# Three edits and a new order in a one-core transformer block: shared score tile for two query blocks, scaling within the centring, comparisons on VectorE

## The chip, the core and the metric

The kernel runs on one core of one Trainium2 chip. Its time is the device time of one execution in microseconds. The engines are TensorE (PE in the profile, PEld for its weight loads), VectorE (DVE), ScalarE (ACT), GpSimd (POOL) and SyncE (SP), which issues all the DMAs here. An engine runs its instructions strictly in the order of the program.

## The reference

A transformer block on x of shape (8, 512, 512): attention with 16 heads of 32, then a feed-forward part of two "bit-linear" layers with 2048 hidden columns.

```python
qkv = layernorm(x) @ w_attn + b_attn          # q, k, v; 16 heads of 32; q and k rotated by head
scores = einsum('bhtd,bhsd->bhts', q, k)       # causal: -inf above the diagonal
attn = softmax(scores) * E ** -0.5
x = x + layernorm((attn @ v) @ w_proj + b_proj)

def bitlinear(x, w):
    xn = layer_norm(x)
    g = max(abs(xn))                           # of a row
    x_hat = clip(xn * 128 / g, ...) * g / 128  # no rounding
    w_hat = sign(round(w / mean(abs(w)))) * mean(abs(w))   # -1, 0, 1 times one number
    return x_hat @ w_hat.T
h = gelu(bitlinear(layernorm(x), w_fc))        # 512 -> 2048
x = x + layernorm(bitlinear(h, w_proj))        # 2048 -> 512
```

## The kernel before

Rows are handled in blocks of 128: 8 batches of 4 blocks give 32 blocks. To keep accuracy, a float32 operand of a matmul is split into two float16 halves, a rounded one ("cast") and what is left of it (the "remainder").

The program consists of some twenty streams, each a Python generator that issues a few instructions per step. `ORDER` is a string of 4519 letters; each letter runs the next step of its stream, and every engine keeps exactly that order. So which instruction stands before which on an engine is read from the string.

- `w`, `H`, `J`, `B`, `R`: load and prepare the attention weights. `t`, `T`: load the feed-forward weights in 16 pieces of 128x1024 (twice), and sum their magnitudes. `Y`: thresholds, then for each piece (`ternarize`) two steps: `neg = w < -half` on GpSimd (L443) and `(w > half) - neg` into fp8 on VectorE (L445).
- `n`, `N`: load and normalise a block of x, split and transpose it. `Q`, `V`: queries and keys of four heads (L551, L565), values (L521, L536). One query and key step group is 12 steps.
- `S` (`maxima`): scores of four heads and one of the four query blocks. Query block i sees (i+1)x128 keys. Each unit claims two of the three PSUM tiles of the pool `sc` (2 banks each); twelve matmuls fill them (L583), then VectorE adds the mask, copies to the tile `p` and reduces (L595, two per tile), and adds the two parts of the shift (L605). 12 steps for the four blocks.
- `A` (`probabilities`): Exp on ScalarE (L627), the cast (L632), the remainder on GpSimd (L634), and for blocks 0 to 2 together and for block 3 a transposing DMA (`pT`). 28 steps for the four blocks.
- `W`: attention weights times values (L661), with the end on VectorE (L674 to L680). `G`: split and transpose the result. `P`: project (L706), with normalisation and residual.
- `F`: normalise, scale, split and transpose the rows for the first layer. `X`: the first layer (L782) and Gelu (L791). `Z` (`ff_quantise`, 15 steps a block): mean, centring on GpSimd (L808), largest magnitude (L810), sum of squares on ScalarE (L815), then, with the scale known, cast (L738) and remainder (L740, VectorE) of each half and its transposing DMA. `C`: the second layer (L838, 8 steps of 4 matmuls), normalisation, residual, store.

Small reciprocal square roots run on GpSimd (L151) and stand in the same queue as its large instructions.

Of the kernel before, what the change touches and what calls it, by code (L numbers as in the profile page):

```python
# [10 lines left out]
F32 = mybir.dt.float32  # L11
# [24 lines left out]
nnwwwNBNNnwnttHtJJHHNNHHHNHHwNNBBJINBRJBNBBJBTHNBHHHNJNBTNTBHNNNHNNNwNBRNHtTtTttJJJHHttRRRRwBTNN  # L36
NBtTHNBBNBRRHHTBttTtYRRJTtYTtYTNtNNQJJJJJNTtJRNHQQHJJQTJTwQQQQTYYYYQJHJHHYHttQtQQnSQYQYSSwQYtYtt
QYSHSAYAANSAAtYAAAnAQQQNJYtQQQQQSVAASVJJAJVJAASHSAAAAAQAQQQYVQVNSQAAASVQVQVHSSVVQAAVAVQQQAAAASAS
VSYJVVtVVVVYAVSSVVAAAASAVVVYYAVAAJtVSSQQQQWVWWnnAAQAQWWWAAAQQQNQVVNNNANSNNNNSWWWWWWAAAAAAQANVNAN
WANNWSnSAVAARSSSAAAASSSWYYAAtAVNANSVWWWWSAAAAAAAAWNQNSSGGWWWWWWYYNYAnAAAAAAWVVVWSVSVVQQQVSAAAAAA  # L40
AAQGQSYSGAAASAAGAQSRVRSrWVVAAWtWWtWQSAQWVWSSQQWYRAAWWVYQWSQAAWVWWSYGSAYAAAVAAAAARSQQQQQQQQAQQQSQ
SWtAAAAASASAYWWWGYGAAVAGAWSWWWWWWWWWASAVSGGSVGVQAAAQQAAQAAASAAPYSQPAAAPtPQSPSQASSQAQQAVQVPQFAAVW
WVSVAVFAAVVVAFnSrAYASAPANWPSFWPVPNVSVQFQFWQAWnAQFAAAAAPWWQQQQQQNNNNNWNNSSPNFWWWAAAAAAAASSNWNNAAA
AWGFSAAAPPPNSSNXPPXAAAXXSAFQSSSNANVAVWFFAXrWWWWWXXXXQGNFnWAAAXASQSYYZWZWWNWWAAAAQXSWVZQVAFZZWZAA
XXQYXQQAXXQXPAZZQAnXQSXXPFSQQSQPrSSPPPFANWWWWWWAAGASSGVVrGWAAASWWWWAAAAZAAZAAAZWVSVVZVWWSQQVVSQS
PQAAAAAAAAAQSZQAZZZZSQQAQQVAASQQSFVVVAAAWWCCCASVSAASWGWWGWSGAAAWZSCWCVWCGWWWWAAAAAZAFVFVNSQQSWSQ
NZAAAAQFSSAAACQQAACCSSCCAAQGZZQFZQQQQFVVVVGWGASVAAnWVAVVVWASWWWWCAAArPSSAVAAZCZZFPSWWPWWWWVWVAAA
AXPPXXSSQAASAZAZAAAFAZZQAAAACQXQQFCXQAFnXCXXQXSQQQNNXPNFANCQSSZZNNANNAAAAAASCFWQSCWNNNANACAWWZZn
GCSCCPSSPWWCSGWNPAWWAPAAVNNWNWACXrWPWVAVVVVVWVVVAAAFZSVSVAAXZQZZAXAQVQVQXZVQPFSAAAAVZQZPPFSPFQSS
FFFFAPPFFAAAQAAXXXXQSSXZZCZZFFFFAXPAZZCXQQQSCAZAZZZFZZNAAFFZXCZZZZZZPCPXCXCXAXACXCCCXSSSXCPPPGGG  # L50
WWWWWGWXSSZWAQCAASCCCAAQWWWWWWWACCZSAZFAAAASSAQAACQQCSZZZQFAAAAASAGCCCSZACQQSCZQAQSrAWWWWQWWGWVQ
VCWWWrAWAWAWCWAAAGVGPGVFGZXNASAZVXVXVZFVAVSAXPVXASFPFXAVVAPQZSPPQZSSQAFXAAAAQQQQXQZSZANXCSQCQnPA
AASCWWWAWAWWCFFXQAZAQZFVSZWSCVCAAAAASWSAAVVCWCNFPCZWWZWPSAPACCQnAWZZZQWAPQZXAAZFQXXQCQFAQXQGGSQC
QrSZZANZNPNAAZZAAAXAFXXXACXSSSCXZZXQQSNNSCVCWCWVCWWWWFACAZNZNAZZAAAZXCZSWWWXnFPWNZCWWWAAAnFANNNN
CFNAAVVXXXZWPCXXZSXCPVZPZNNZCXNrSXPNSSXAANZPCVSAAAAAAVCAVCZZCSAASCZVZSZCZAAAAAAVVAAAZFZZCCVVSSCV
VSCXCWXWQWQWnWWQZZPZSVFZPQZAAAPAAAXSQFQPGGGAFQPGQSXQZCrASXFQAAAACWAXFSAQPAXCSWWWWCWQQPCFQWXCAZZA
SAZAZWSSZAZAACSQAACQAZZCFSWCQQQWQWWWnFSWQAAANFXGGQCWXWXWWAZCSAAAAZZFNCQFGFAQWXAWXWCrCWAAXFVFXSFS
ZXVXSGVVVSZQGVXQAFQAZXZVGAZAVASQQQQXSAQVQSZAAAAAAZQQXVFZXSQPFZVVPWPPAZSAZAZCZWFFPCVCZZWWWCWPFXWF
FZCVCAASSAASACACCAZAZZXCCAAASSXXXCACAVVPXSPZSSQAArPQZZPPAAAAAQQQZQSCZFFWWWZWWAACQAWSSQZWZCQPCAQN
NAAAAASQQAAAAGANCXGCFNSNNNSZCCSCXWVWWWZWWWCCNVWWXZWWWWWAXAnAAnPVVZZSSPSZAVAAPVPNVSVAANNFSNCrCASC  # L60
CNAAAAAAANNNFFAAAXAAPNXCXCXCXVCVFZXSVSCFXSZSFSXCVWQXFWQXQAZAZWWWWCAPAACZSAZACPZAXXQPCCZXZrXFZFQA
ZZPGGZGQWXQXSQPQWWZZZSNWFGAPWCASQAACAAAQAZAZAASCFSWCWQCVWSCAZSSFZZACVAAAACVVCXCSQCQSQAZAAAFnAGQS
ZGQQZGQQPnWWQWWAWSQWAAAAAACWVWWWWWWWArXNVZSNQXCFFQGGAGSSAVAXVPZSSZQQQPAASFAAXAAQQPXFAQPFQXQSQPVA
QZSAXVXAWAWAQAQVZZSXZVVAZVSAZVVCVAWFWCSWACWZZFFZVCZWVWZWCWWVWWAAAPZSZCWZZSAAAASnAAZASCXZZCXXASQA
QQCCCAAAACQQQQCXXQACQCQNNNCACXNSSCSFNQCNNAFANNFQPACPANNANAAAFSSNCPPAFSZCPSAXXCCXASGGAWWrWWWWAAVX
WSNVNnWWWWZWWSNAAZAFWAFVVVXVSXXSQXZZAZAAZVVAAAAZZZSZZACrAAQQQQAZQSPPAZZAAAAXXPXZXQPQNPFAXQCAPCXS
QFSCQZXPZCSSXAQAVCSVZZZZAXAZACZSAAVVXZZCPSZFAAPAFCZSPWXCWXWWWPWXXZASAnAZGZCFCGGFCCFWWXWCWCWFWFAX
PSQASSCFQZGWWQAAAAAAACZQCSQQCSAAAAQQZSSQFANAArASWQQFQCFGWCASZAZVCCVWWWVVGWWWGWVWWAWWCCWVAAAAVVVC
SrCASFASVVVVAXZZPGGAGVAZVVXSQAXSAQPQXPAFAAFFZZSQPFZAZAAANNAQQAXXPXXQPZZZXFFXPZQZPQSSQSQQPFSPZWPn
CWWAAAAAWWCAnWPCSVSSVCAAWAAAAAZAVSSXCZVSQQQQAAAZAAZXZCZAQASZZZQQWQWWQWQNNANCSZZNNNNNWQXQAWWAAAFA  # L70
ANNACCXCNNNACXCANCCCCCSSAAACSASAACZFSASCAVCCXSXSXWWWWWWNAAANXAGGSWWWWWWWVrAXSCFACQAQVAFFWZFFVASA
PQXQQQQXZASQAZPAQAAASSSPQZPXAZQQAAAPAAZVSPZSAFVVZVAAVCAArSXZVXXZCFVZZVPZZVFXXVVXXVXZPXZSSXPWWXCW
FZAZZZCAZPGCXWCPCGGWCZZZSZWZZCXZCXXZPWZGSAXAACAAAAAACCCCAQCSWWCWWWCQFWXCZSSZCQCAAAAACAFCZZZFFWQG
AFFSWSZZSAZWWWQCWWCQVrACGGSWQVQXQACACASSZZXXAAAQSWAWZAASZAWAAXAAQXAAXWFWXWQZXFWXZVFVSQFQGXCZPZAS
AQSWZQQQFCrSACQAWAQACFAFAAQZSCGQGQCFCZZQVSAVCZAAAAWWWWVZZVPCCXZFAPWFFAASPFSZXZPPXVSAAZPXXXFFVCZX
XAACVPXZPSVCCrPXFZXPFSZZFSCXCXAASPQAXZCQCQCAZZZFQAFZZSWWAWAACZZZZZXZXPCWFXQXWQSXAFFAPWACAZFXFFCC
FPSPPCWAAAZAASPSrZCQWQZZZZWAQQAAQQCAASZZSSACAPCZPWCWSAZSWCWACCCZAASSAGGWCPAAAPSAWWWAPWWWCCCAAZAG
SAXAAVWXXVASZZASAFFSAAGAAXAVXXArAXCXFXSPXZCCCZWWCZASCVWWZWWZZZZCSZGWAGXAASZZZAASAAAFAASAXCCSXFZS
SXFAAAZZCPWAWWZWFWAAAAAAAAWAFFCWCXFGCCCXCXXXCCXZZFFZZZXZCXXGFFWCXXXWXWWWWCWWWWWWWrGWZGGXGCCXZXZZ
ZZCZXXXZZZPZCXXXCCPPZZPPZPFXPFFCXrCFZFPZCPFZCPCXXPPFCPCZZZZZPXZZCXXPXZZXXPCFCCCrCCZPFFXFCXFCXZZZ  # L80
ZZZCPFFZXPFCFZZZPZZZFFCXZCXCCXZCPCXXPXFZZZZFFZZPCrCZCPXZFZFCXCZXXXFFCZXZCZXCZXFZXCZXZZFZFZZZZZZC
CCCZCCCXXCXXCXCXCXZCZZZZZZZZZZZZZXXCXCZCZCCCCCXCXCXXZZCZZZZCCZCZZZZZCCCZCZCZCCCCCCCCCCCCCCCCCCCC
CCCCCCC
# [4 lines left out]
def block_kernel(  # L88
# [349 lines left out]
    def ternarize(n, i):  # L438
        dst = piece((wfc, wout)[n], i)
        t = pcs.pop((n, i, 1))  # L440
        half, nhalf = thr[n]
        neg = tp.tile(list(dst.shape), BF16, tag="q", name="neg", bufs=2)
        nc.gpsimd.tensor_scalar(neg, t, nhalf, None, ALU.is_lt)  # L443
        yield
        nc.vector.scalar_tensor_tensor(  # L445
            dst, t, half, neg, ALU.is_gt, ALU.subtract, saturate=False
        )
        yield
# [119 lines left out]

    def maxima(u):

        b, g = divmod(u, NG)
        src = srcs.pop((b, g))
        low = lows[u % 2]
        nm = small.tile([P, NT, 4], F32, tag="nmax", name="nmax")
        for i in range(NT):
            n = (i + 1) * P
            scs = [sc_tile(), sc_tile()]
            for m, (hq, hk) in enumerate(((0, 3), (2, 3), (0, 1))):  # L580
                for j in range(4):
                    rows = slice(j * HD, (j + 1) * HD)
                    nc.tensor.matmul(  # L583
                        scs[j // 2][:, j % 2, :n],
                        src[rows, hq, ts(i, P)],
                        src[rows, hk, :n],
                        start=(m == 0),
                        stop=(m == 2),
                    )
            yield  # L590
            for t in range(2):
                p = pp.tile([P, 2, n], F32, tag="p", name="p", bufs=3)
                scores[2 * u + t, i] = p, nm[:, i, 2 * t : 2 * t + 2]
                for j in range(2):
                    nc.vector.tensor_tensor_reduce(  # L595
                        p[:, j, :],
                        scs[t][:, j, :n],
                        mask[:, T - n :],
                        e_scale[:, g : g + 1],
                        3.0e38,  # L600
                        ALU.add,
                        ALU.min,
                        low[:, i, 2 * t + j, 0:1],
                    )
                nc.vector.tensor_reduce(  # L605
                    nm[:, i, 2 * t : 2 * t + 2], low[:, i, 2 * t : 2 * t + 2], AX.X, ALU.add
                )
                yield

# [5 lines left out]
    def probabilities(u):  # L615

        qs = {}
        for i in range(NT):
            part = PARTS[i]
            for t in range(2):  # L620
                if STARTS[i] == 0:
                    shape = [P, 2, 2, BLOCKS[part] * P]
                    qs[t] = pp.tile(shape, F16, tag=f"ph{part}", name="ph", bufs=2)
                q = qs[t]
                p, add = scores.pop((2 * u + t, i))
                for j in range(2):
                    nc.scalar.activation(  # L627
                        p[:, j, :], p[:, j, :], AF.Exp, bias=add[:, j : j + 1], scale=-1.0
                    )
                yield  # L630
# [368 lines left out]
```

## Time and profile before

| | |
|---|---|
| runs | 1089.4, 1091.85, 1092.23 us; median 1091.85 us |
| profiled execution, its own time | 1095.54 us |
| its span, first to last instruction | 1093.7 us |
| mean granted TensorE clock | 0.973 |
| busy: PE, DVE, ACT, POOL | 987.7, 965.6, 870.4, 766.7 us |
| matmuls | 8170 |
| DMA traffic | 189.77 MB, mean 174 GB/s |

PE's busy time is modelled from pipelined matmuls, so a matmul's own duration (381 ns for 512 columns) is longer than the distance to the next one. In a waits list a line names who waited, for whom, the sum in us, how often and the longest. In a timeline a line gives the start, the length, the engine, the line of the kernel, the operation, what it writes and reads, and how many; in brackets stands the idle time before it and what ended it. L-numbers are lines of the kernel before.

### The profile page before, as it was taken

To read this page: it belongs to the slowest core of one execution; us is meant where nothing else is said; L and a number is where in the kernel's file an instruction comes from. 1 tells how busy PE (TensorE), PEld (TensorE's weight loads), DVE (VectorE), ACT (ScalarE), POOL (GpSimd) and SP (SyncE) were. 2 spreads that over 40 slices of the span, in tenths; PEclk is the share of its full clock that TensorE was granted. 3 is DMA by queue.
4 is the path that set the end of the run, shared out by engine and by line. 5 is a ranking of instruction groups with operands and counts; after the bars stand their busy time and mean duration, and the time that the engine had idled before them with its cause. 6 is when DMAs were issued, how large, how long until landed. Compare 5 with 4: busy or idle time off the path is not lost. (4 is left out here: it accounts for less than half of the span.)

```text
span 1093.7 us, 23185 instructions
## 1 busy us (share of the span) xinstructions
PE 987.7 (90%) x8170; PEld 502.3 (46%) x8170; DVE 965.6 (88%) x2859; ACT 870.4 (80%) x1439; POOL 766.7 (70%) x678
## 2 busy tenths in 40 slices
PE   2668577898999999999999999999999999999996
PEld 1325334445454554545454554445454444444442
DVE  6988889998989998999799988999999989987964
ACT  4747777698888898998879898998899879974551
POOL 6888998887785767866577858777784666763533
PEclk9889799999999999999999999999999999999999
DMA  9657998999998999998799999999997989995653
GB/s 311 215 187 161 180 209 156 191 173 171 185 169 165 176 191 170 188 188 160 145 179 190 189 159 188 174 184 166 181 181 164 173 155 160 167 195 112 136 108 89
DMA packets 588501, 189.77 MB, mean 174 GB/s; under 512 B 564576, under 2 KB 568672, under 8 KB 588384
## 3 DMA queue, kind: packets, MB, share of 16 engines
q1 hardware_dynamic: 588384, 188.28, 88.6%
q8 instruction: 64, 1.05, 0.4%
q14 instruction: 53, 0.43, 0.1%
HBM read 38.29 MB, written 8.39 MB: 43 GB/s over the span
## 5 line engine op out<-in xcount | busy, mean ns | idle before, releaser
L634 POOL TENSOR_TENSOR ph<-p,ph 128x256 f16<-128x256 f32 (+3 forms) x256 | 372.4, 1461 | 128.7 <-ACT ph L632 109.2
L627 ACT ACTIVATE p<-p,nmax 128x384 f32<-128x384 f32 (+3 forms) x512 | 258.3, 552 | 36.1 <-DVE nmax L605 34.2
L595 DVE CUSTOM_DVE_ANT_0 p<-sc,mask,e_scale 128x384 f32<-128x384 f32 (+3 forms) x512 | 260.0, 545 | 16.7 <-PE sc L583 8.7
L838 PE MATMUL mm<-wout,qT 128*128 128x512 fp8e4 x1024 | 256.6, 381 | 3.4 <-DMA qT<-q 3.2
L782 PE MATMUL sc<-wfc,qT 128*128 128x512 fp8e4 x1024 | 255.8, 381 | 2.4 <-ACT h L791 2.1
L551 PE MATMUL mm<-xT,wqk 128*128 128x512 f16 x768 | 202.4, 391 | 6.3 <-DVE sc L676 2.5
L632 ACT CAST ph<-p 128x256 f16<-128x256 f32 (+3 forms) x256 | 184.8, 722 | 10.3 <-DMA pT<-ph 4.3
L782 PEld LDWEIGHTS <-qT 128*128 128x128 f16 x1024 | 96.8, 98 | 116.4 <-issue 12.3
L838 PEld LDWEIGHTS <-qT 128*128 128x128 f16 x1024 | 94.6, 98 | 110.1 <-issue 6.7
L661 PEld LDWEIGHTS <-pT 128*128 128x128 f16 x2560 | 94.0, 97 | 54.1 <-issue 14.3
L551 PEld LDWEIGHTS <-wqk 128*128 128x128 f16 x768 | 71.4, 100 | 96.0 <-issue 25.6
L661 PE MATMUL sc<-vt,pT 128*128 128x65 f16 (+1 forms) x2560 | 97.5, 187 | 17.3 <-DMA pT<-ph 8.5
L521 PE MATMUL mm<-wv,xT 128*128 128x256 f16 x768 | 104.8, 280 | 7.5 <-DVE src L565 4.9
L583 PE MATMUL sc<-src 32*128 32x128 f16 (+3 forms) x1536 | 86.2, 303 | 26.6 <-DVE low L595 16.1
L706 PE MATMUL mm<-wp,oT 128*128 128x512 f16 x384 | 103.1, 384 | 0.8 <-DMA oT<-hT 0.8
L740 DVE SCALAR_TENSOR_TENSOR q<-h,hqs,q 128x1024 f16<-128x1024 f32 x64 | 84.7, 1333 | 10.0 <-ACT q L738 9.9
L808 POOL TENSOR_SCALAR h<-h,hnm 128x1024 f32<-128x1024 f32 x64 | 74.5, 1168 | 26.7 <-DVE hnm L803 25.3
L521 PEld LDWEIGHTS <-xT 128*128 128x128 f16 x768 | 74.5, 100 | 35.4 <-issue 13.5
L791 ACT ACTIVATE h<-sc,fsc 128x1024 f32<-128x1024 f32 x64 | 71.2, 1113 | 17.8 <-PE sc L782 11.4
L738 ACT ACTIVATE q<-h,hqs 128x1024 f16<-128x1024 f32 x64 | 72.3, 1141 | 14.5 <-DMA qT<-q 7.0
L810 DVE TENSOR_REDUCE htop<-h 128x1 f32<-128x1024 f32 x64 | 76.5, 1210 | 5.8 <-POOL h L808 5.7
L815 ACT ACTIVATE junk<-h 128x1024 bf16<-128x1024 f32 x64 | 67.3, 1051 | 16.9 <-POOL h L808 12.1
(152 smaller groups left out, 1384.0 us busy)
## 6 DMA issues: line engine op xcount, KB each, us to landing
row<-in_x SPq DMA_DIRECT2D x32, 256.0 KB, 3.4
tw<-in_w_fcT SPq DMA_DIRECT2D x16, 512.0 KB, 4.9
tw<-in_w_outT SPq DMA_DIRECT2D x16, 512.0 KB, 4.9
x<-in_x SPq DMA_DIRECT2D x32, 256.0 KB, 3.3
out<-row SPq DMA_DIRECT2D x32, 256.0 KB, 3.1
wraw<-in_w_attn SPq DMA_DIRECT2D x8, 256.0 KB, 4.6
pT<-ph SPq DMA_TRANSPOSE x128, 5.6
qT<-q SPq DMA_TRANSPOSE x96, 4.4
```

The source lines that it names most:

```text
L521: nc.tensor.matmul(ps[:, :256], xT[:, c, hx, k, :], wv[hw][:, k, half * 256 : (half + 1) * 256], start=(n == 0), stop=(n == 3 * NE - 1),)
L551: nc.tensor.matmul(ps, w[:, hw, k, :], xT[:, :, hx, k, :], start=(n == 0), stop=(n == 3 * NE - 1),)
L583: nc.tensor.matmul(scs[j // 2][:, j % 2, :n], src[rows, hq, ts(i, P)], src[rows, hk, :n], start=(m == 0), stop=(m == 2),)
L595: nc.vector.tensor_tensor_reduce(p[:, j, :], scs[t][:, j, :n], mask[:, T - n :], e_scale[:, g : g + 1], 3.0e38, ALU.add, ALU.min, low[:, i ...
L627: nc.scalar.activation(p[:, j, :], p[:, j, :], AF.Exp, bias=add[:, j : j + 1], scale=-1.0)
L632: nc.scalar.copy(hi, p)
L634: nc.gpsimd.tensor_tensor(lo, p, hi, ALU.subtract)
L661: nc.tensor.matmul(oo[:, j, i, :width], probs[u, PARTS[i]][:, half, j, STARTS[i] + c, :], vt[c][:, h, :width], start=(n == 0), stop=(n == ...
L706: nc.tensor.matmul(ps, oTs[b, k][:, ho, i, :], wp[hw][:, k, :], start=(n == 0), stop=(n == 3 * NE - 1),)
L740: nc.vector.scalar_tensor_tensor(q[:, 1], rows, s, q[:, 0], ALU.mult, ALU.subtract)
L782: nc.tensor.matmul(ps[:, o1, :], xsT[0][:, n // NE, n % NE, :], wfc[:, n % NE, ts(o, 512)], start=(n == 0), stop=(n == 2 * NE - 1),)
L838: nc.tensor.matmul(ps, hT[0][:, half, k, :], wout[:, o2 * NF // 2 + k, :], start=(n == 0), stop=(n == 2 * NF - 1),)
```

## The change

Three edits, and a new `ORDER` of 4263 letters.

1. `maxima` and `probabilities`: query blocks 0 (128 keys) and 1 (256 keys) are written next to each other into the same PSUM tiles and the same `p` tile. Their reductions and Exps stay separate; the last small reduction, the cast and the remainder are done once for both (384 columns per head). An S group has 9 steps, an A group 24.
2. `ff_quantise`: the largest magnitude is taken of Gelu's output before centring; the scale is half of what the largest value would allow; the centring on GpSimd multiplies by the scale as well. Cast and remainder then need no scale; the remainder of the first half is a subtraction on VectorE, that of the second on GpSimd. The square sum comes behind the half's transposing DMA. 14 steps a block.
3. `ternarize`: the comparison runs on VectorE.

```diff
 ORDER = """
...
 """
...
-        nc.gpsimd.tensor_scalar(neg, t, nhalf, None, ALU.is_lt)
+        nc.vector.tensor_scalar(neg, t, nhalf, None, ALU.is_lt)
...
+    UNITS = (((0, 0), (1, P)), ((2, 0),), ((3, 0),))
...
-        for i in range(NT):
-            n = (i + 1) * P
+        for n, blocks in enumerate(UNITS):
             scs = [sc_tile(), sc_tile()]
...
+            for i, at in blocks:
+                for m, (hq, hk) in enumerate(((0, 3), (2, 3), (0, 1))):
+                    for j in range(4):
+                        rows = slice(j * HD, (j + 1) * HD)
+                        nc.tensor.matmul(
+                            scs[j // 2][:, j % 2, at : at + (i + 1) * P],
...
+            end = at + (i + 1) * P
             for t in range(2):
...
+                p = pp.tile([P, 2, end], F32, tag="p", name="p", bufs=3)
+                scores[2 * u + t, n] = p, nm
+                for i, at in blocks:
+                    for j in range(2):
+                        nc.vector.tensor_tensor_reduce(
...
+                i0, i1 = blocks[0][0], blocks[-1][0] + 1
                 nc.vector.tensor_reduce(
-                    nm[:, i, 2 * t : 2 * t + 2], low[:, i, 2 * t : 2 * t + 2], AX.X, ALU.add
+                    nm[:, i0:i1, 2 * t : 2 * t + 2], low[:, i0:i1, 2 * t : 2 * t + 2], AX.X, ALU.add
                 )
                 yield
...
+                for i, at in blocks:
+                    for j in range(2):
+                        pj = p[:, j, at : at + (i + 1) * P]
+                        nc.scalar.activation(
+                            pj, pj, AF.Exp, bias=nm[:, i, 2 * t + j : 2 * t + j + 1], scale=-1.0
+                        )
+                    yield
+                end = STARTS[last] + last + 1
+                hi, lo = (q[:, h, :, STARTS[first] * P : end * P] for h in range(2))
                 nc.scalar.copy(hi, p)
                 yield
                 nc.gpsimd.tensor_tensor(lo, p, hi, ALU.subtract)
                 yield
...
-        nc.scalar.activation(q[:, 0], rows, AF.Copy, scale=s)
-        yield
-        nc.vector.scalar_tensor_tensor(q[:, 1], rows, s, q[:, 0], ALU.mult, ALU.subtract)
+        if s is None:
+            nc.scalar.copy(q[:, 0], rows)
+        else:
+            nc.scalar.activation(q[:, 0], rows, AF.Copy, scale=s)
+        yield
+        if s is None:
+            eng.tensor_tensor(q[:, 1], rows, q[:, 0], ALU.subtract)
+        else:
+            nc.vector.scalar_tensor_tensor(q[:, 1], rows, s, q[:, 0], ALU.mult, ALU.subtract)
         yield
...
     def ff_quantise(b, c):
         hTs, eps, h, hsum = ff[b, c]
         nm = tiny(name="hnm")
+        hsq, htop, top = tiny(2, "hsq"), tiny(2, "htop"), tiny(name="htop1")
+        for o2 in range(2):
+            nc.vector.tensor_reduce(
+                htop[:, o2 : o2 + 1], h[:, ts(o2, 1024)], AX.X, ALU.max, apply_absolute_value=True
+            )
+            yield
+        nc.vector.tensor_reduce(top, htop, AX.X, ALU.max)
+
+        s = scale_of("h", top, Q_S / 2)
         nc.vector.tensor_scalar(nm, hsum[:, 0:1], hsum[:, 1:2], -1.0 / FF, ALU.add, ALU.mult)
         yield
...
         for o2 in range(2):
             hh = h[:, ts(o2, 1024)]
-            nc.gpsimd.tensor_scalar(hh, hh, nm, 1.0, ALU.add, ALU.mult)
...
+            nc.gpsimd.tensor_scalar(hh, hh, nm, s, ALU.add, ALU.mult)
+            yield
+            yield from quantised_T(hh, None, hTs[o2], nc.gpsimd if o2 else nc.vector)
             junk = tp.tile([P, 1024], BF16, tag="q", name="junk", bufs=2)
             nc.scalar.activation(junk, hh, AF.Square, accum_out=hsq[:, o2 : o2 + 1])
             yield
...
-        for o2 in range(2):
-            yield from quantised_T(h[:, ts(o2, 1024)], s, hTs[o2])
...
+        s2 = tiny(name="hs2")
+        nc.vector.tensor_scalar(s2, s, s, EPS_BIT, ALU.mult, ALU.mult)
         nc.vector.tensor_scalar(eps, hsq[:, 0:1], hsq[:, 1:2], 1.0 / FF, ALU.add, ALU.mult)
-        nc.vector.tensor_scalar(eps, eps, EPS_BIT, gqs[1], ALU.add, ALU.mult)
-        nc.vector.tensor_scalar(eps, eps, s, s, ALU.mult, ALU.mult)
+        nc.vector.tensor_scalar(eps, eps, s2, gqs[1], ALU.add, ALU.mult)
         yield
```

All letters of `ORDER` are new; its counts per stream change only for S (384 to 288), A (896 to 768) and Z (480 to 448).

## The prediction

> **What bounds the kernel now.** I read the windows by engine first, then the waits of the start-up and of the rest, then the timeline of the tail. All durations are of the one profiled execution: span 1093.7 us, its own time 1095.54, which is 3.7 above the median of the runs shown (1091.85). Differences are worked out in that execution and taken off the median. A measurement of this kernel tells about 0.3% from no change, some 3.3 us.
>
> The windows: each row is a stretch, its length, then busy us (and instructions) of PE, PEld, DVE, ACT and POOL, the granted PE clock, the DMA share, GB/s.
>
> ```profile
> 0.00:50.00 50.00, 20.76 (x83) 11.94 (x84) 39.71 (x108) 28.64 (x49) 34.90 (x55) 0.94 0.82 274
> 50.00:175.00 125.00, 88.95 (x874) 49.83 (x872) 108.25 (x329) 85.29 (x158) 114.96 (x79) 0.85 0.81 181
> 175.00:300.00 125.00, 110.94 (x1085) 58.86 (x1083) 115.08 (x364) 103.65 (x183) 96.69 (x80) 0.97 0.95 176
> 300.00:525.00 225.00, 220.57 (x1859) 112.07 (x1858) 208.56 (x635) 201.72 (x327) 158.78 (x144) 1.00 0.95 177
> ...
> 550.00:950.00 400.00, 394.35 (x3380) 199.81 (x3379) 369.22 (x1123) 359.44 (x586) 285.24 (x251) 1.00 0.97 175
> ...
> 1075.00:1093.70 18.70, 8.77 (x32) 3.43 (x32) 5.87 (x15) 0.00 (x0) 5.90 (x6) 0.86 0.38 94
> ```
>
> From 300 to 950 us TensorE is 98 to 99% busy at full clock. In its densest stretch 52 matmuls of 512 columns take 11.39 us, 0.22 each, back to back, so nothing that helps another engine shortens these stretches. What can move is the start-up (50 to 300 us: PE idle 50 of 250), some scattered waits and the tail. Who ends PE's waits in the start-up:
>
> ```profile
> PE sc L583 <- DVE low L595: 13.8, 12, 2.7
> PE sc L661 <- DVE low L595: 5.4, 5, 2.3
> PE mm L521 <- DVE src L565: 4.9, 4, 1.8
> PE sc L583 <- DVE on L680: 4.1, 4, 2.1
> ...
> PE sc L661 <- DMA pT<-ph: 2.5, 2, 1.6
> ```
>
> VectorE ends nearly all of them, although it is itself idle for 26.7 of these 250 us (250 - 108.25 - 115.08). What ends DVE's idle there:
>
> ```profile
> DVE p L595 <- PE sc L583: 5.3, 3, 3.3
> DVE p L595 <- POOL ph L634: 3.2, 5, 1.4
> DVE vt L536 <- ACT vt L534: 2.4, 3, 1.4
> ...
> DVE row L717 <- POOL hT L508: 0.9, 1, 0.9
> ```
>
> GpSimd ends 5.1 us of it (3.2, 0.9, and 0.5 each by hT at L595 and by neg at L445). From 50 to 175 us POOL is fuller than DVE (114.96 against 108.25), and 40.6 of POOL's busy time there are 14 of the 16 comparisons of L443. So DVE is the start-up's bound and POOL a close second that delays it.
>
> The tail: the last rows' quantisation, and the contraction that waits for it.
>
> ```profile
> 1066.64 2.21 POOL L808 TENSOR_SCALAR h<-h,hnm 128x1024 f32<-128x1024 f32 x2
> 1067.80 2.35 DVE L810 TENSOR_REDUCE htop<-h 128x1 f32<-128x1024 f32 x2 [2.35 <-POOL h L808]
> ...
> 1072.00 1.28 DVE L740 SCALAR_TENSOR_TENSOR q<-h,hqs,q 128x1024 f16<-128x1024 f32 x1 [1.27 <-ACT q L738]
> ...
> 1073.35 4.52 SPq L499 DMA_TRANSPOSE qT<-q  x2
> ...
> 1077.79 1.83 PE L838 MATMUL mm<-wout,qT 128*128 128x512 fp8e4 x5 [3.24 <-DMA qT<-q]
> ```
>
> PE stands 3.24 us until the first transpose lands. The matmuls after it run to about 1086.6 without a gap, so this wait is on the path to the end.
>
> **The change, part by part.** No matmul is added or taken away, nor a transpose; 24 score matmuls stand before the first wait instead of 12 and 12.
>
> *Comparisons to VectorE.* POOL loses 16 x 2.896 = 46.3 us, all before 230 us. DVE gains 16 comparisons of 128x1024 f32. Bounds: 0.43 us each (L301, a scalar operation on half the width, 427 ns) and 1.42 (L445, two inputs at full width). The line through 154 ns (L719, one element) and 427 ns (512) gives 0.70, which I take: +11.2 us (ends 6.8 and 22.7). It lies on the engine that bounds the start-up. Each comparison stands in DVE's own queue in front of L445; queued behind are the score reductions (L595), on which PE waits.
>
> *Blocks 0 and 1 together.* ACT: 64 x (0.402 + 0.615 - 0.829) = -12.0 us. POOL: 64 x (0.711 + 1.223 - 1.679) = -16.3. DVE: 64 small reductions of 157 ns go and the 64 that stay get a little longer, say -0.15 each, -9.6 in all. The exponentials of block 0 now wait for block 1's reduction, some 1.1 us later (2 x 0.478 + 0.157); ACT, 80% busy, covers that in the dense stretches. In the start-up it can cost 1 us for each of about 10 groups at worst, but one PSUM pair less is claimed per group, in the place where PE waits longest (13.8 us), so I take nothing.
>
> *Second layer.* DVE loses 32 remainders of 1.333 = -42.7; the other 32 become a plain subtraction, between 1.21 (L810, one input) and 1.33: 0 to -3.9. POOL gains 32 x 2.230 (L634 at 128x1024) = +71.4. The centring takes a second column operand: L480 against L761 (884 and 786 ns) says +0.1 for 64 instructions, +6. ACT: 64 x (1.141 - 1.042) = -6.3. The order alternates between Exp and Gelu four times more (72 against 68): 4 x 1.283 = +5.1.
>
> *Totals.* DVE 965.6 + 11.2 - 9.6 - 44 = about 923; POOL 766.7 - 46.3 - 16.3 + 77 = 781; ACT 857; PE unchanged. From 300 us on only a wait can matter.
>
> *Start-up by count.* At about 300 us of before the 132nd Q step is done. Up to it the new order has nearly the same steps of every stream that feeds PE (V 94 and 94, P 26 and 26, X 20 and 20, W 121 and 121). DVE's load up to there: comparisons +11.2; score groups -4.5 (before 117 steps of 12 per group of 11.3 us, after 86 of 9 per group of 11.0: -2.9 for the reductions saved, the rest a slight lag); three F steps fewer -1.4; quantisation -1.6. Sum +3.7. POOL's load up to there falls by 50. I take the 5.1 us that DVE waited for POOL as gone and the rest of its idle as it is: -1.4 for the start-up. Bounds: half of the 26.7 idle gone, with the load at its lowest (3.7 - 4.4), gives -14; idle unchanged and the load at its highest (3.7 + 11.5) gives +15.
>
> *Middle.* After 300 us the waits list shows PE waiting 3.8 us on DVE, 4.1 on Gelu (ACT) and 6.0 on pT transposes. DVE is 4% lighter, so I take 2 of the 3.8. POOL's longer remainder (2.23 for 1.33) and what is queued behind it (square roots L151, the score remainders L634, and SP's transposes that wait for those) cost nothing as long as POOL has room: 285 of 400 us, and 32 us more of work in such a stretch (77/966 x 400) makes 79%.
>
> *Tail.* Before, from the last Gelu's end (1064.5) to the first transpose (1073.35) 8.9 us pass. Afterwards: one reduction 1.21 (the first half is reduced while the second Gelu runs), small operations 0.7, centring 1.2, cast 1.04, subtraction 1.25 and gaps 0.4: 5.8, so 3 us sooner. The second half: cast behind the square 1.24, POOL 2.23: 9.2, before 11.1. After the last X step the new order also leaves 24 contraction steps of 0.87 us on PE, before 21: 2.6 us more cover. The 3.24 go: -3.2.
>
> *A rule against it.* L740 reads two SBUF tensors; in 64 runs its median is 1282 ns, its mean 1333, while POOL is 70% busy. Contention is thus 0.05 us each, 3 us over all, and the change keeps that price. The Trainium skill (SBUF — State Buffer, Who interferes with whom) says that a VectorE operation with two SBUF inputs, or in a two-port mode, and a GpSimd operation that reads SBUF exclude each other for the whole instruction. By it each comparison could wait out a score remainder of 2.2 us, and the start-up would be up to 16 x 2.2 = 35 us longer, an estimate from that page; the L740 row does not show such waits.
>
> Sum: -1.4 - 2 - 3.2 = -6.6, 1091.85 - 6.6 = about **1085**. This case's own range is 1078 to 1088.5.
>
> **The rivals.**
> *VectorE pays for the comparisons (slower).* Place: 50 to 175 us, where PE waits for L595. Its idle stays at 26.7 us because it comes from PE and ACT, not POOL (the named waits give POOL only 5.1). Price: 3.7 at 0.70 us a comparison, 15 at 1.42; less the tail's 3: +1 to +12, 1093 to 1104, likeliest 1098. It decides once the idle shrinks by less than about 3 us, or a comparison costs over 1 us.
> *GpSimd becomes late (slower).* Remainders of 2.2 us in one queue with square roots and score remainders: the 6.0 us of PE waiting for pT become three times as long, +12 - 3: about 1100. For it: ph waits already end with POOL. Against: 79% load.
> *Nothing arrives.* PE is at its pace for 800 us, the start-up gains nothing and the tail's gain is eaten by new waits: 1090 to 1094.
> *More comes.* Half of DVE's idle goes (-10) and the waits on DVE and Gelu with it (-6), tail -3: 1072.
>
> **How the numbers follow.** Forecast 0.43, more 0.10, nothing 0.14, comparisons 0.20, GpSimd 0.13. Faster 0.53, same 0.14, slower 0.33. The range reaches from 1072 to 1103, leaving out the extremes of both sides.
>
> **What would show it.** Comparisons near 0.70 us on DVE; DVE's idle from 50 us to the 132nd Q step (22 of L565) near 22 us; that point at about 298 us; DVE busy 923, POOL 781, ACT 857; no PE wait for qT in the tail. Wrong: PE waits for L595 above 19 us in the start-up, comparisons over 1 us, or PE waits for pT that grow beyond 10 us.

## The result, and the profile after

The changed kernel takes 1098.83 us (median of 10 runs, 1096.3 to 1103.21) against 1092.32 (10 runs of the kernel before): ratio 1.0067, 95% interval 1.0047 to 1.0087. It is 0.7% slower where 0.6% faster was forecast. The profiled execution took 1096.79 us with a span of 1095.0, 2 us under its median. The kernel before was profiled a second time (span 1090.6); where it is used below it is called "before, again".

The windows by engine of the kernel after, columns as in the prediction:

```profile
50.00:175.00 125.00, 90.50 (x923) 50.98 (x923) 118.55 (x341) 84.53 (x150) 80.75 (x56) 0.87 0.87 180
175.00:300.00 125.00, 109.81 (x1088) 59.24 (x1089) 114.23 (x364) 103.76 (x177) 95.55 (x71) 0.99 1.00 187
...
550.00:950.00 400.00, 388.38 (x3323) 198.50 (x3322) 352.50 (x1076) 350.98 (x557) 304.19 (x236) 1.00 0.95 173
...
975.00:1075.00 100.00, 95.03 (x472) 42.75 (x468) 66.78 (x155) 43.05 (x66) 50.00 (x46) 0.98 0.56 113
1075.00:1095.00 20.00, 8.94 (x32) 3.36 (x32) 4.33 (x12) 1.15 (x2) 6.85 (x6) 0.87 0.30 77
```

From 50 to 300 us VectorE is busy 232.8 us where it was 223.3. In the stretch from 975 to 1075 us, where little but the last layer is left, TensorE is at 95% (99.17 of 100 in before) at a clock of 0.98 (1.00 in before). The totals are 932.3 for DVE, 781.0 for POOL and 855.1 for ACT.

Busy shares hide where a few microseconds go, so I used one more view, worked out from the trace. Each matmul is counted at the distance to the next one that its kind has in dense stretches (0.2165 us for 512 columns); all 8170 make 965 us in every kernel here. "Lost" at time t is t less the matmuls done by then at that price.

| lost us by | 300 | 900 | 1050 | end | from 900 to the end |
|---|---|---|---|---|---|
| before | 110.7 | 113.2 | 116.2 | 128.7 | 15.5 |
| before, again | 110.7 | 111.3 | 114.9 | 125.6 | 14.3 |
| after | 103.3 | 107.3 | 116.4 | 130.0 | 22.7 |

So in this execution the start-up gained 7.4 us, five times what was predicted. The middle gave back 1.5 to 3.4, and all the rest of the loss lies behind 900 us: 7 to 8 us, of which 5.5 to 6.1 between 900 and 1050 and 1.1 to 2.9 behind 1050.

One execution is not the whole story. Three versions below differ from after only in the last eight blocks, behind 900 us. In their profiled executions about 0.4, 2.8 and 3.9 us more than in after are lost by 300 us, and -0.2, 1.3 and 1.3 more by 900. So the start-up's gain was 3 to 7 us, and the middle's loss is not clear of this spread. That the profiled execution of after was a quick one is also why the ends in the table differ by only 1.3 and 4.4 us where the medians differ by 6.5.

The timeline of the tail after (start, length, engine, line, what it writes and reads, count; in brackets the idle time before it and what ended it):

```profile
1061.58 1.11 ACT L806 ACTIVATE h<-sc,fsc 128x1024 f32<-128x1024 f32 x1
...
1063.97 1.06 ACT L835 ACTIVATE junk<-h 128x1024 bf16<-128x1024 f32 x1 [1.19 <-DMA qT<-q]
...
1065.15 0.21 DVE L842 TENSOR_SCALAR hsc<-hsq 128x1 f32<-128x1 f32 x1 [2.95 <-ACT junk L835]
...
1065.59 2.33 DVE L820 TENSOR_REDUCE htop<-h 128x1 f32<-128x1024 f32 x2
...
1074.89 1.26 POOL L872 TENSOR_TENSOR row<-row,x 128x512 f32<-128x512 f32 x1 [0.93 <-DVE row L870]
...
1076.11 2.12 POOL L753 TENSOR_TENSOR q<-h,q 128x1024 f16<-128x1024 f32 x1
1076.66 3.63 PE L853 MATMUL mm<-wout,qT 128*128 128x512 fp8e4 x16 [1.96 <-DMA qT<-q]
...
1082.57 5.31 PE L853 MATMUL mm<-wout,qT 128*128 128x512 fp8e4 x16 [2.28 <-DMA qT<-q]
```

Read it from the top. The last Gelu (L806) ends at 1062.8 with its accumulator. VectorE should then be reducing, but its queue holds L842 of the row block before, which wants that block's square (L835), and the square wants a buffer of tag `q`, which the transpose of that block's first half still holds until it lands. VectorE stands idle for 2.95 us. Then POOL's remainder (L753) stands behind an addition (L872) that waits for another block's result. TensorE waits twice, 1.96 and 2.28 us, where it waited once, 3.24 us, in before; and its last 16 matmuls take 5.31 us instead of 3.63.

### The profile page after: what moved, and what is told of

It is laid out like the page before. It is cut to its first block, busy times and chain, and to the rows that moved or that the text cites. A ratio compares the mean times of both kernels' runs of the same rounds, so it can differ in the third digit from the quotient of the medians.

```text
span 1095.0 us, 22861 instructions
## 1 busy us (share of the span) xinstructions
PE 973.4 (89%) x8170; PEld 499.7 (46%) x8170; DVE 932.3 (85%) x2779; ACT 855.1 (78%) x1379; POOL 781.0 (71%) x630
## 5 line engine op out<-in xcount | busy, mean ns | idle before, releaser
L642 POOL TENSOR_TENSOR ph<-p,ph 128x768 f16<-128x768 f32 (+1 forms) x192 | 360.9, 1883 | 101.9 <-ACT ph L640 91.5
L634 ACT ACTIVATE p<-p,nmax 128x384 f32<-128x384 f32 (+3 forms) x512 | 253.7, 551 | 21.4 <-DVE nmax L608 19.4
L597 DVE CUSTOM_DVE_ANT_0 p<-sc,mask,e_scale 128x384 f32<-128x384 f32 (+3 forms) x512 | 255.5, 546 | 9.2 <-POOL ph L642 6.4
L640 ACT CAST ph<-p 128x768 f16<-128x768 f32 (+1 forms) x192 | 172.8, 900 | 4.1
L853 PEld LDWEIGHTS <-qT 128*128 128x128 f16 x1024 | 94.6, 98 | 118.9 <-issue 16.6
L831 POOL TENSOR_SCALAR h<-h,hnm,hqs 128x1024 f32<-128x1024 f32 x64 | 83.6, 1307 | 45.7 <-DVE hnm L827 43.4
L669 PE MATMUL sc<-vt,pT 128*128 128x65 f16 (+1 forms) x2560 | 100.7, 186 | 14.4 <-DMA pT<-ph 10.2
L518 PE MATMUL mm<-wv,xT 128*128 128x256 f16 x768 | 101.5, 273 | 6.6 <-DVE src L562 2.9
L748 ACT CAST q<-h 128x1024 f16<-128x1024 f32 x64 | 66.6, 1041 | 45.9 <-POOL h L831 38.8
L583 PE MATMUL sc<-src 32*128 32x128 f16 (+3 forms) x1536 | 77.6, 302 | 27.4 <-DVE low L597 15.8
L835 ACT ACTIVATE junk<-h 128x1024 bf16<-128x1024 f32 x64 | 67.3, 1051 | 27.6 <-DMA qT<-q 27.1
L753 POOL TENSOR_TENSOR q<-h,q 128x1024 f16<-128x1024 f32 x32 | 69.1, 2161 | 22.1 <-ACT q L748 18.9
L806 ACT ACTIVATE h<-sc,fsc 128x1024 f32<-128x1024 f32 x64 | 71.0, 1110 | 6.7 <-PE sc L797 6.2
```

The costliest lines, as they stand in the source:

```text
L518: nc.tensor.matmul(ps[:, :256], xT[:, c, hx, k, :], wv[hw][:, k, half * 256 : (half + 1) * 256], start=(n == 0), stop=(n == 3 * NE - 1),)
L583: nc.tensor.matmul(scs[j // 2][:, j % 2, at : at + (i + 1) * P], src[rows, hq, ts(i, P)], src[rows, hk, : (i + 1) * P], start=(m == 0), st ...
L597: nc.vector.tensor_tensor_reduce(p[:, j, at : at + (i + 1) * P], scs[t][:, j, at : at + (i + 1) * P], mask[:, T - (i + 1) * P :], e_scale[ ...
L634: nc.scalar.activation(pj, pj, AF.Exp, bias=nm[:, i, 2 * t + j : 2 * t + j + 1], scale=-1.0)
L640: nc.scalar.copy(hi, p)
L642: nc.gpsimd.tensor_tensor(lo, p, hi, ALU.subtract)
```

## The experiments

Every ratio is to the kernel before, with the 95% interval. Diffs are against the changed kernel unless said otherwise.

**Is the square's claim on a buffer to blame, or GpSimd's long remainder? First try: move the work.**

```diff
-            junk = tp.tile([P, 1024], BF16, tag="q", name="junk", bufs=2)
-            nc.scalar.activation(junk, hh, AF.Square, accum_out=hsq[:, o2 : o2 + 1])
+            nc.scalar.activation(hh, hh, AF.Square, accum_out=hsq[:, o2 : o2 + 1])
```

> The changed kernel, but ScalarE's square of the centred half (L835) is written over the half itself instead of into a scratch tile that turns through the same two buffers as q; nothing else differs. Theory A (the square, now behind its half's transposing DMA, waits for a q buffer that this DMA still reads: ScalarE 27 us of waits for qT against 2 before, VectorE 19 us at L842): those waits fall below 8 us and the time falls by 4 to 8 us, to 1091 to 1095. Theory B (GpSimd's longer queue delays the transposes): within 2 us of the changed kernel. Theory C (comparisons on VectorE): within 2 us.

Measured: 1119.34 us, 1.0257 [1.0235, 1.0280]. The expected gain turned into a loss of 20 us: the square now overwrites what the remainder still reads, so ScalarE waits for the remainders instead of for the transpose: 36.2 us in 18 waits for GpSimd's, 16.6 in 13 for VectorE's.

```diff
-            yield from quantised_T(hh, None, hTs[o2], nc.gpsimd if o2 else nc.vector)
+            yield from quantised_T(hh, None, hTs[o2], nc.vector)
```

> The changed kernel, but the second half's remainder on VectorE too (32 subtractions of 1.22 us on VectorE, 32 of 2.16 us less on GpSimd); order unchanged. Theory B: PE's waits for pT and the spread of the runs shrink, the time falls by 4 us or more. Theory A: within 2 us. Theory D (VectorE and GpSimd exclude each other when both read SBUF: VectorE's instructions ran 37 us over their medians, before 24): the excess falls below 30 us and the time by 2 to 4.

Measured: 1125.14 us, 1.0320 [1.0298, 1.0342]. DVE's busy time rises to 971.6 us and TensorE has lost 145 us by 1050, most of the rise between 300 and 900 us. Neither edit says anything on the cause: each moves work to a place in the queues for which `ORDER` was not written, and that price (20 to 26 us) is larger than what was to be measured.

**What did the comparisons alone do?** Two runs cross the one edit that stands apart from the others: the changed kernel with comparisons back on GpSimd, and the kernel before with comparisons on VectorE.

```diff
-        nc.vector.tensor_scalar(neg, t, nhalf, None, ALU.is_lt)
+        nc.gpsimd.tensor_scalar(neg, t, nhalf, None, ALU.is_lt)
```

> The changed kernel, but the 16 comparisons on GpSimd again, at the same places of the order. Theory C (VectorE pays for the comparisons in the start-up): faster by 4 us or more. Theories A, B, D and the profile (at 300 us PE stands 8 us further than before): slower by 3 to 10 us, since GpSimd gets 46 us more before 230 us in an order that does not reckon with it.

> The kernel before with only its 16 comparisons on VectorE, order unchanged. Theory C: slower by 5 to 12 us. Otherwise between 6 us faster and 2 us slower: VectorE's load to 300 us grows by 11 us, GpSimd's falls by 46.

Measured: comparisons back on GpSimd 1115.96 us, 1.0222 [1.0202, 1.0241]; the old order with them on VectorE 1105.04 us, 1.0127 [1.0104, 1.0150]. Lost by 300 us is 125 and 123.6, against 103.3 in after and 110.7 in before, and behind 300 us nothing changes. The edit alone, in the old order, costs the start-up 13 us; together with the new order it is part of a gain of 3 to 7. Both runs put the comparisons where their order was not written for them, so neither gives the comparisons' own price in the changed kernel.

**Second try: take work out where it stands.** The place in the queues stays, only the suspected length goes. In the first two GpSimd subtracts 512, or 2, of the second half's 1024 remainder columns and fills the others with zeros; in the other two the square takes 16 columns, once still in a buffer of tag `q`, once in a 32-byte tile of its own. To make room for that tile, six small tiles that serve to prepare the attention weights have one buffer instead of two.

```diff
-            eng.tensor_tensor(q[:, 1], rows, q[:, 0], ALU.subtract)
+            if eng is nc.gpsimd:
+                eng.tensor_tensor(q[:, 1, :512], rows[:, :512], q[:, 0, :512], ALU.subtract)
+                eng.memset(q[:, 1, 512:], 0.0)
...
-            nc.scalar.activation(junk, hh, AF.Square, accum_out=hsq[:, o2 : o2 + 1])
+            junk = small.tile([P, 16], BF16, tag="junk", name="junk", bufs=1)
+            nc.scalar.activation(junk, hh[:, :16], AF.Square, accum_out=hsq[:, o2 : o2 + 1])
```

> The changed kernel, but GpSimd makes only the first 512 columns of the second half's remainder and fills the other 512 with zeros (that part of the remainder is left out): about 1.7 us instead of 2.16 on GpSimd, 32 times, order unchanged. Theory B (GpSimd's length delays what is queued behind): 2 to 5 us faster than the changed kernel. Theory D (exclusion of VectorE's two-input operations while GpSimd reads): 1 to 4 us faster, VectorE's excess over its medians, 37 us, falls to about 31. Theory A (the square's buffer): within 2 us.

> The changed kernel, but of the second half's remainder GpSimd makes only 2 columns and fills the other 1022 with zeros (left out): about 1.6 us, as long as in the run beside it, but hardly any reading. Theory D: VectorE's excess falls below 28 us and it is at least 2 us faster than the run with 512 columns. Theory B: the same time as that run. Theory A: within 2 us of the changed kernel.

> The changed kernel, but the square covers only 16 of 1024 columns (the rest of the square sum is left out) and still claims a q buffer: ScalarE loses 64 x 0.84 us of work, its waits for qT stay. Theory A: the time stays within 3 us of the changed kernel. If ScalarE's load is the matter: 5 us or more faster.

> As the run beside it (square of 16 columns, the rest left out), but with a buffer of its own of 32 bytes, so that it claims no q buffer and waits for no transposing DMA. Theory A: at least 4 us faster than that run, ScalarE's waits for qT at L835 gone, and about 1090 us or less. Theories B, D: the same as that run.

| edit | median us | ratio to before | less than after |
|---|---|---|---|
| 512 columns of remainder | 1091.85 | 0.9988 [0.9970, 1.0007] | 7.0 |
| 2 columns of remainder | 1090.35 | 0.9973 [0.9957, 0.9989] | 8.5 |
| square of 16 columns, buffer of `q` | 1097.29 | 1.0038 [1.0019, 1.0057] | 1.5 |
| square of 16 columns, tile of its own | 1093.65 | 1.0005 [0.9988, 1.0021] | 5.2 |

The last column compares medians of different groups of runs; the kernel before, measured beside each group, stayed between 1092.16 and 1092.89 us. Both suspects cost something. Of the square's 5.2 us 3.6 belong to the buffer (the difference of the last two rows; 4 or more were expected); the other 1.5 are not clear of noise. Half of GpSimd's columns bring nearly all of its gain, which speaks against a cost that grows with GpSimd's load (busy 781.0 us with all columns, 762.7 with half, 747.0 with 2). But the fill was shorter than expected (0.95 us, and 0.23 for the 2 columns, where 1.6 in all was expected), so these two versions do not separate reading from length, and the 1.5 us between them are not clear of noise.

How GpSimd's remainder costs is seen in one place. The timeline of after near 999 us:

```profile
998.85 0.55 POOL L148 TENSOR_TENSOR pr<-pr,mhalf 128x1 f32<-128x1 f32 x1 [2.87 <-DVE pr L727]
...
999.37 2.13 POOL L753 TENSOR_TENSOR q<-h,q 128x1024 f16<-128x1024 f32 x1
999.43 2.61 DVE L731 SCALAR_TENSOR_TENSOR x<-row,pr,x 128x512 f32<-128x512 f32 x1 [0.48 <-POOL pr L148]
...
1011.88 3.25 PE L853 MATMUL mm<-wout,qT 128*128 128x512 fp8e4 x8 [2.81 <-DVE row L870]
```

GpSimd's small square root releases VectorE's addition to `x1` (L731). GpSimd's own next instruction, the remainder, starts 60 ns ahead of it. The addition takes 2.61 us instead of 0.75 and ends half a microsecond after the remainder. VectorE's queue is late by that much down to L870, which frees the PSUM tile for TensorE: a wait of 2.81 us, and then 8 matmuls in 3.25 us that elsewhere take 1.89. With 2 columns and the fill, the same place:

```profile
997.13 0.20 POOL L754 TENSOR_TENSOR q<-h,q 128x2 f16<-128x2 f32 x1
997.20 0.75 DVE L731 SCALAR_TENSOR_TENSOR x<-row,pr,x 128x512 f32<-128x512 f32 x1 [0.48 <-POOL pr L148]
997.26 0.95 POOL L755 MEMSET q<- 128x1022 f16 x1
...
1007.79 1.89 PE L857 MATMUL mm<-wout,qT 128*128 128x512 fp8e4 x8 [0.95 <-DVE row L874]
```

The fill reads nothing, runs beside the addition for 0.7 us, and the addition is at its 0.75. At this place 1.86 us of wait and 1.36 of slow matmuls are saved, 3.2 of the 8.5 us.

**Only in the last eight blocks.** Since the loss lies behind 900 us, the two moves of the first try were repeated for the last two batches alone, singly and together.

```diff
+            yield from quantised_T(hh, None, hTs[o2], nc.gpsimd if o2 and b < 6 else nc.vector)
+            junk = hh
+            if b < 6:
+                junk = tp.tile([P, 1024], BF16, tag="q", name="junk", bufs=2)
```

> The changed kernel, but in the last 8 of the 32 blocks (two of eight batches, quantised after about 950 us) the second half's remainder is on VectorE. Theory E (the loss lies after 900 us, where no attention work is left to cover the longer chain reduce, scale, centre, cast, remainder, transpose of a block, and GpSimd's remainder is on that chain; VectorE is only two thirds busy there): 3 to 7 us faster than the changed kernel. Theory B' (GpSimd's remainders cost all over the run, evenly): 8/32 of the 8.6 us that halving them brought, about 2 us. If the order alone is at fault, off-order work makes it slower, as with all 32 (+26).

> The changed kernel, but in the last 8 blocks the square is written over the centred half and claims no q buffer. Theory E with A (in the last 100 us the chain stands twice on the square that waits 4.3 us for a transposing DMA): 3 to 6 us faster than the changed kernel. Otherwise slower by 1 to 5, a quarter of the +20 that this did in all 32 blocks, since the square then waits for GpSimd's remainder.

> Both edits of the two runs beside it in the last 8 blocks. Theory E: 6 to 11 us faster than the changed kernel, so 1088 to 1093, level with the kernel before or a little faster. Otherwise no faster than the changed kernel.

Measured: 1101.88, 1.0082 [1.0059, 1.0104]; 1100.83, 1.0072 [1.0047, 1.0097]; 1101.32, 1.0076 [1.0052, 1.0099]. All three miss: 2 to 3 us above after, not below (the intervals overlap with after's). With the remainder on VectorE a wait of 3.6 us for L533 appears between 950 and 1000 us that was not there. Moving work does not give the cost back even where the engines have the most room.

> The kernel before, unchanged, for a second profile: its first profiled execution took 3.7 us more than the median of its runs. Expected 1092; PE's idle time to 300 us, 50 of 250 us in the first profile, shows whether those 3.7 us lay in the start-up.

The kernel before once more: 1092.09 us, 0.9994 [0.9980, 1.0007]. Its lost time by 300 us is the same, so the first profile's 3.7 us did not lie in the start-up; 1.9 lay in the middle and most of the rest behind 1050 us.

**Edits that keep all the work and its place.** There are still two readings: GpSimd's remainder holds VectorE's addition up while both read (called held ports below), or GpSimd is merely late, since a shorter remainder also makes GpSimd earlier. So the same 1024 columns were subtracted in two instructions; and the second half's square was written over the first half of `h`, whose remainder is long done.

```diff
+            if eng is nc.gpsimd:
+                for w in range(2):
+                    c = slice(w * 512, (w + 1) * 512)
+                    eng.tensor_tensor(q[:, 1, c], rows[:, c], q[:, 0, c], ALU.subtract)
...
+            if o2:
+                junk = h[:, :1024]
+            else:
+                junk = tp.tile([P, 1024], BF16, tag="q", name="junk", bufs=2)
```

> The changed kernel, GpSimd's remainder of the second half done in two instructions of 512 columns, one behind the other: all the work is there and GpSimd's time is 32 short instruction starts longer. Theory G (held ports): VectorE's addition to x1 (L731) is held for the length of one GpSimd instruction, so it should now be held about half as long: longest case 1.6 us where 2.6 was, its excess over the median 4 to 6 us where 10.6 was, and the time 2 to 6 us under the changed kernel. Theory L (GpSimd is merely late: the half remainder of 512 columns helped because GpSimd had a microsecond less to do per block): nothing is gained, 0 to +3 us.

> The changed kernel, the square of the second half of h written over the first half of h, whose remainder VectorE has long taken, in place of a buffer of tag q: half of the square's claims on q go, and nothing new is waited for. Theory Q (the square's buffer costs its share, about 3.6 us for two claims per block by the two runs with a square of 16 columns): 1 to 3 us under the changed kernel, and the tail loses the square's wait for the last transpose but one. Rival (the order fits the claims as they are, as with the square in place): 0 to +10 us.

> Both edits of the two runs before at once: GpSimd's remainder in two instructions, the second half's square written over the first half of h. All the work is there. If both costs are real and lie in different places: 3 to 9 us under the changed kernel, so 1090 to 1096 us. If the order absorbs only one of them, it equals the better of the two.

> Both suspects taken away together: GpSimd subtracts 2 columns of the second remainder and fills the rest with zeros, and the square takes 16 columns into a small tile of its own. The remainder's columns and 1008 columns of each square are left out. If the two costs behind 900 us are separate, the gains add up: 8.5 and 5.2 us, so about 1085 us, which is also where the prediction's time was. If one hides the other: 1088 to 1090 us.

| edit | median us | ratio to before | less than after |
|---|---|---|---|
| remainder in two instructions | 1093.95 | 1.0011 [0.9994, 1.0027] | 4.9 |
| second square over `h` | 1094.46 | 1.0018 [1.0003, 1.0033] | 4.4 |
| both | 1092.78 | 1.0005 [0.9988, 1.0021] | 6.1 |
| 2 columns, and square of 16 in a tile of its own | 1084.24 | 0.9940 [0.9921, 0.9958] | 14.6 |

The split answers it for a part. GpSimd's busy time rises by 6 us, to 787, and yet the kernel is 4.9 us faster. The timeline of the same place:

```profile
1000.29 2.71 POOL L756 TENSOR_TENSOR q<-h,q 128x512 f16<-128x512 f32 x2
1000.35 1.63 DVE L731 SCALAR_TENSOR_TENSOR x<-row,pr,x 128x512 f32<-128x512 f32 x1 [0.49 <-POOL pr L148]
...
1011.84 1.89 PE L858 MATMUL mm<-wout,qT 128*128 128x512 fp8e4 x8 [1.85 <-DVE row L875]
```

The addition gets in after the first of the two instructions: 0.98 us shorter, TensorE's wait 0.96 us shorter, and the 8 matmuls are back at 1.89. That is 2.3 of the 4.9 us (of which 1.36 the slow matmuls, which do not follow every such wait, see the end); the rest I could not pin to one place. My bound for L731's total was off: its mean falls only from 1082 to 1012 ns, an excess over its median of 8.3 us, not 4 to 6. Of the twelve additions in after that took over 0.9 us only three stand beside this remainder (2608, 2607 and 1932 ns; 1635, 1632 and 1750 in the split); the others stand beside instructions of GpSimd that the split leaves as they are. What counted was the one that a wait of TensorE hung on. For the 3.6 us by which 2 columns gain more than the split, both readings stay open.

The two edits that keep the work gain 4.9 and 4.4 us alone and only 6.1 together; whether the order absorbs the rest is open. In the last row, with both suspects gone, the gains add up (8.5 and 5.2 expected, 14.6 measured). That its time, 1084.24 us, is 0.8 from the predicted 1085 is luck: this version leaves work out, and its stages are not those of the sum. Its lost time by 900 us is 105.8, and from 900 us to the end it loses 11.4 where after loses 22.7. Its tail has one wait:

```profile
1065.73 0.20 POOL L756 TENSOR_TENSOR q<-h,q 128x2 f16<-128x2 f32 x1
1065.86 0.95 POOL L757 MEMSET q<- 128x1022 f16 x1
1066.84 2.88 SPq L498 DMA_TRANSPOSE qT<-q  x1
1071.45 3.63 PE L859 MATMUL mm<-wout,qT 128*128 128x512 fp8e4 x16 [0.90 <-DMA qT<-q]
```

Of the versions that do all the work, the one with both edits comes out level with the kernel before (the interval holds 1), and none beats it. It was not tried with these edits in the last eight blocks alone, so that they act there rather than earlier rests on the table of lost time. No run takes the shared score tile or the new order alone either, so what these add to the loss is not shown.

## Why the prediction was wrong

**Start-up: direction right, term mis-sized.** Predicted -1.4, measured -7.4 in the profiled execution and -3 to -7 over four. The score groups' term should have been about -5 by its own figures (117/12 groups of 11.3 us less 86/9 of 11.0), not -4.5, which is 0.5 of the gap. Up to the 22nd L562 VectorE's idle time from 50 us fell to 12.9 us (22 predicted, 25.6 in before), and that point came 5.4 us sooner, at 279.4 against 284.8; I had put it at 300 in before. (In the three versions that share this start-up the idle time was 13.4 to 15.6 us and the point came at 279.6 to 283.1.) Only 5.1 us of idle had GpSimd's name on it and I took those alone as gone; its idle time behind PE and ACT shrank too. That those in turn had waited for GpSimd is likely, since the comparisons back on GpSimd bring the idle time up to 40 us, but the order differs as well. A comparison took 0.746 us at the median and 0.913 on average (14.6 us in all, 11.2 predicted), inside the limit of 1 us that I had set. PE's waits for L597 add up to 16.9 us in the start-up, under 19. The rival in which VectorE pays for the comparisons is refuted in the place that it named, though its time (1098) is what was measured.

**Middle: no gain.** Predicted -2, measured +1.5 to +3.4 in this execution, about -1 to +3 over the four. VectorE was lighter, but the waits for pT went to 8.1 us from 6.0:

```profile
PE sc L669 <- DMA pT<-ph: 8.1, 9, 1.7
PE mm L853 <- DMA qT<-q: 4.2, 2, 2.3
PE mm L714 <- DVE vt L533: 3.6, 1, 3.6
PE mm L853 <- DVE row L870: 2.8, 1, 2.8
```

That is the waits list of TensorE from 300 us on (sum, times, longest). 8.1 is below the 10 at which I called GpSimd late. The third and fourth lines are new. The third, one wait of 3.6 us near 385 us, is as large as the middle's whole loss; the second and fourth lie behind 900 us. (The prediction's "98 to 99%" left out 525 to 550 us, where PE was busy 22.66 of 25 us.)

**Tail: a step that failed.** "The 3.24 go: -3.2." Measured behind 1050 us: +1.1 to +2.9. I let 5.8 us pass from the last Gelu's end to the first transpose, with the first half's reduction beside the second Gelu. In the trace 9.5 pass (1062.8 to 1072.3), because both reductions stand behind L842 in VectorE's queue, L842 behind the square, and the square behind the transpose that holds its buffer. The diff showed that the square, which had stood ahead of the block's casts, now claims its buffer between and behind them, from a tag that has two, so that a transpose must land first. I named the engine that does the reduction and not what stands ahead of it in its queue. The second half was to be out 9.2 us after the Gelu and was 15.5: the late first half, and GpSimd's remainder behind L872.

The other versions bear the chain out. From the last Gelu to the first transpose 9.5 us pass in all four that keep the square and both its claims (after, 512 columns, 2 columns, the split), 8.25 in both with the second square over `h`, and 7.4 in both with a square of 16 columns in a tile of its own, where the 27.1 us that ScalarE's square waited for qT in after are gone:

```profile
1061.47 0.19 ACT L808 ACTIVATION_READ_ACCUMULATOR h<-sc,fsc 128x1 f32 x1
...
1069.07 1.68 SPq L498 DMA_TRANSPOSE qT<-q  x1
...
1079.39 3.63 PE L855 MATMUL mm<-wout,qT 128*128 128x512 fp8e4 x16 [1.70 <-DMA qT<-q]
```

A short square that keeps its claim has 7.5 too, so the square's length counts as well. The 1.6 us that are left over 5.8 are mostly the first reduction: the order puts it behind L842, and so behind the second Gelu, even then.

**900 to 1050 us: the other step that failed, and the larger one.** The sum holds nothing for GpSimd's long remainder: it was to "cost nothing as long as POOL has room", and for contention "the change keeps that price". The stage lost 5.5 to 6.1 us more than in before. Leaving out all but 2 of the remainder's columns makes the kernel 8.5 us faster, 4.3 of it in this stage of the profiled executions; with both suspects gone the stage loses as little as in before. I had read L740's mean of 1333 against a median of 1282 ns as a price of 0.05 us. That was the wrong row: L740 is not the operation that GpSimd releases, and a mean over 64 is no bound for the one on the path. Nor is it true that the row shows no such waits: its longest was 2220 ns. In after the rows are these (shortest, median, longest in ns):

```profile
L731 DVE SCALAR_TENSOR_TENSOR x<-row,pr,x x32: 741/754/2608, 183.4 to 1033.1; 128x512 f32<-128x512 f32 x32
...
L440 DVE TENSOR_SCALAR neg<-tw,tnhalf x16: 742/746/2623, 53.8 to 234.5; 128x1024 bf16<-128x1024 f32 x16
```

Both have cases that last as long as a GpSimd remainder. In before the same addition went over 0.9 us in two of 32 cases (1443 and 992 ns), in after in twelve, and each of the twelve ended 0.54 or 0.55 us after a GpSimd instruction that had started before it. The Trainium skill (SBUF — State Buffer, Who interferes with whom) says just this: the one that issues second is blocked until the first has finished, and an instruction that only writes does not block one with two inputs. The runs agree: 2.61 us beside a remainder of 2.13, 1.63 beside one of half the columns, 0.75 beside the fill. My estimate from it of up to 35 us for the comparisons is not borne out; they exceeded their median by 2.7 us in all. The price that TensorE saw fell on the operation that GpSimd itself releases.

**GpSimd becomes late** was the nearest rival in mechanism: place and cause lie with GpSimd's long remainder. But where the split gained, GpSimd was not late: it held VectorE. The rival's 1100 was reached by another way.

## What to carry to other kernels

Where a short GpSimd operation releases a VectorE operation with two SBUF inputs, look at GpSimd's next instruction: if it is long and reads SBUF, it can start first (60 ns ahead here), and the VectorE operation then lasts as long as it; cutting it in two gave 4.9 us back here. When a step moves behind a DMA and claims a buffer, follow the buffer to its release and list all that stands behind the waiting instruction in its queue, and then behind that. To test a cost in a program with a fixed order, shorten the work where it stands: edits that move it cost 2 to 26 us here for suspects worth 5 to 9.

## What the runs showed of the hardware

A short wait of TensorE can cost more than itself. After the wait of 2.81 us in after the next 8 matmuls took 3.25 us instead of 1.89, at a granted clock of 0.53; after 2.00 and 2.09 us, in the two versions with the remainder on VectorE in the last eight blocks, 3.50 and 3.44; after 1.85 us in the split version 1.89. The Trainium skill (TensorE: Matmul & The Clock Gate, Part 1: The HAM clock gate (the "warmup" mystery)) gives half speed after an idle window of about 3.4 us; here shorter waits were enough. But length alone doesn't decide. The kernel before shows it best: its last 32 matmuls stood behind the same wait in both profiles, and only in the first did they slow down (granted clock 0.81 and 1.00):

```profile
1077.79 8.77 PE L838 MATMUL mm<-wout,qT 128*128 128x512 fp8e4 x32 [3.24 <-DMA qT<-q]
...
1076.38 7.08 PE L838 MATMUL mm<-wout,qT 128*128 128x512 fp8e4 x32 [3.22 <-DMA qT<-q]
```

Likewise the version with a square of 16 columns in its own tile kept 1.89 us for 8 matmuls behind a wait of 2.81. And in the version with the second square over `h` the last 16 matmuls kept full speed behind a wait as long as the 2.28 that cost after 1.7 us:

```profile
1083.81 3.63 PE L856 MATMUL mm<-wout,qT 128*128 128x512 fp8e4 x16 [2.30 <-DMA qT<-q]
```

What decides is not shown. Since two executions of one kernel differ in it, the 1.4 us behind the wait near 1012 us and the 1.7 us at the end of after are in part chance.
